# A graph layer on one core: units of picks that run on across groups, and a batch's copy in the middle of an iteration

## The chip, the cores and the metric

The kernel runs on one core of one Trainium2 chip. The metric is the device time of one execution in microseconds (us); the median of several executions is given, and a profile of one execution, taken apart from them, shows the work of the engines: PE (TensorE) multiplies matrices into PSUM, DVE (VectorE) and ACT (ScalarE) work elementwise, POOL (GpSimd) issues the gathers by index, and SP (SyncE) issues the other DMAs.

## The reference

There are N = 6250 nodes with 64 features, and E = 206250 edges sorted by destination. Four heads of 16 features each; every edge has its own 64 features.

```python
Qh = (x @ Wq.T + bq).reshape(n, H, D)
Kh = (x @ Wk.T + bk).reshape(n, H, D)
Vh = (x @ Wv.T + bv).reshape(n, H, D)
Ee = (edge_attr @ We.T + be).reshape(-1, H, D)
score = (Kh[src] * Qh[dst] * (1.0 / np.sqrt(D)) * Ee).sum(-1)
score = jnp.exp(jnp.clip(score, -5.0, 5.0))
msg = Vh[src] * score[..., None]
wV = jax.ops.segment_sum(msg, dst, num_segments=n)
...
x = _layernorm(x + wV.reshape(n, H * D))
```

So every edge needs the keys and values of its source, the query of its destination and its own projected features; its message is added to the row of its destination, and each row is normalised at the end.

## The kernel before

A prologue multiplies the nodes by the weights and writes a table of keys and values, a table of queries and a table of destination keys to DRAM. Then the edges run in tiles of 128, eight tiles to a group: 202 groups (NG), one iteration of the main loop (L1014) for each, and one more. Two groups make a step for the sums, but for the last eight.

**One iteration g, by engines.** VectorE multiplies keys by queries times edge values and reduces them to scores (`products`), multiplies edge values and queries of the next group (`terms`), adds the last step's sums into a ring of rows (`add`, in every other iteration; `add_blocks` now and then), builds one-hot matrices for the picks of the next iteration (`hots`), forms the message (`message`), and near the end the one-hots of the destinations (`onehot_edges`) and the message's low part (`take`). ScalarE turns scores to weights (`weigh`), adds the edge bias (`biased`, tile eb), copies the message's high part (`keep`), widens one-hots that VectorE wrote in bf16 (`widened`, pieces 1, 3 and 5 of 7) and prepares the one-hots for the queries of group g+4 (`onehot_rows`, `onehot_rows_rest`). PE turns the next group's terms (`turn`, four transposes into qe), multiplies the queries' one-hots (`queries`, into the bank qq), sums a step's messages (`sums`, into `pa`) and multiplies the edges of group g+3 (`edges`, into `ee`). SP fetches edges, keys, query windows, and index rows of sources; POOL gathers keys and values from the table by source index, each lot released by a mark in PE's order (list `where`).

**Picks.** Most tiles get their keys and values by the gather. Four tiles of a batch, two each in two later groups, get them by matmul instead: `picks` selects the sources' rows of x by one-hot matrices, and a product with the weights (`picked_kv`) makes keys and values of them. There are LAST = 78 batches. A batch goes through all nodes in 13 units of 512; a unit is two matmuls (high and low part) into each of two PSUM banks, px[0] and px[1]; the last unit is one into each. Two units make a piece, the seventh piece has one; `hots` makes a piece at a time, in a ring of six buffers. The first unit of a batch starts the accumulation in the banks, the last one ends it.

When a batch is complete, VectorE's `picked` (L722, L723) copies both banks to SBUF, tiles x0 and x1, and chooses by the source's low bits on the way. In the next iteration ScalarE fills the bank qq with the bias (`biased_kv`, L733), PE multiplies x0 and x1 by the weights into it (`picked_kv`), ScalarE copies the result out to the gathered tiles (`place_kv`, L739), and only then may `queries` use qq again.

**Order of the batches.** Batches last three and two iterations in turn (LENGTHS); BEGIN and READY hold each batch's first and last iteration. `pieces_of(g)` deals whole pieces to the iterations of a batch, 2, 2 and 3 pieces or 3 and 4, so that iterations have 4, 4, 5, 6 and 7 units and no iteration holds units of two batches. The loop's `todo` is the list of units of g and `ahead` the pieces of g+1.

In PE's order an iteration runs two units, the turn, the queries, then the other units with the sums between them (after the units where g is in READY), and the edge products at the end. Behind a READY iteration `picked_kv` follows the turn, and the queries come after the sums. `picked` stands at the very end of VectorE's order in a READY iteration, behind `onehot_edges` and `take`. `fetch_sources` (L252) brings the next batch's source indices to one buffer, one iteration before `sources` (two activations, L257 and L258, and a VectorE instruction, L259) turns them to what `hots` and `picked` read; `sources` stands at the end of a batch's first iteration.

**PSUM.** Eight banks: still (constants and a small sum), room (two banks in one tile: `ee` for the edge products, `pa` and `folded` for sums and folds in the other), px[0], px[1], qq, and qe twice. The program's semaphores follow its tiles.

Of the kernel before, what the change touches and what calls it, by code (L numbers as in the profile page):

```python
# [8 lines left out]
F32 = mybir.dt.float32  # L9
# [8 lines left out]
P = 128  # L18
# [79 lines left out]


def pieces_of(g):  # L100

    for m in range(LAST):
        if BEGIN[m] <= g <= READY[m]:
            n, k = READY[m] - BEGIN[m] + 1, g - BEGIN[m]
            return [(m, p) for p in range(len(PIECES) * k // n, len(PIECES) * (k + 1) // n)]
    return []

# [42 lines left out]
def tile_gnn(ctx: ExitStack, tc: tile.TileContext, x, x_blocks, by_rows, xT, wT, bias, beT, weT, eT, src, src_rows,  # L150
# [502 lines left out]
    with tc.If(rv == 0) as branch:  # L653

        with tc.tile_pool(name="work", bufs=2) as work, \
# [9 lines left out]
                                half_b[:2 * UNITS].to_broadcast([2 * UNITS, P]), ident_b[:2 * UNITS, :2 * UNITS])  # L665
            room = fixed.tile([P, 2, 4 * P], F32, name="room")
            ee = room[:, 0].rearrange("p (i e) -> p i e", e=P)
            pa = room[:, 1, :2 * PA]
            folded = room[:, 1, 2 * PA:2 * PA + 2 * C].rearrange("p (b c) -> p b c", c=C)
            sum_ = still[:, 2 * P:2 * P + C]  # L670
# [343 lines left out]
            for g in range(NG + 1):  # L1014
                now, before = g < NG, g > 0
                todo, ahead = [(m, p, u) for m, p in pieces_of(g) for u in range(*PIECES[p])], pieces_of(g + 1)
                going, where = [], []
# [8 lines left out]
                if g % LG == 0 and g + 3 * LG < NG:  # L1026
                    fetch_edges(g // LG + 3, work, 3)
                if g + 1 in BEGIN[1:]:
                    fetch_sources(BEGIN.index(g + 1) + 1, work)
                if g + 4 < NG:  # L1030
# [48 lines left out]
                if g - 1 in ends and now:  # L1079
# [3 lines left out]
                    else:  # L1083
                        short.append(lambda: sums(s))
                for k in range(max(len(todo), 3)):
                    for one in todo[k:k + 1]:
                        picks(*one)
                        where.append(mark[-1])
                    if k == 1:
                        if g + 1 < NG:  # L1090
                            turn(g + 1)
                        if g - 1 in READY:
                            picked_kv(READY.index(g - 1))
                            place_kv(READY.index(g - 1))
                        elif g + 2 < NG:
                            queries(g + 2)
                    if k in (2, 4) and short and g not in READY:
# [5 lines left out]
                if g + 3 < NG:  # L1103
# [218 lines left out]
```

## Time and profile before

| | |
|---|---|
| runs | 2001.13, 2002.62, 1995.0 us; median 2001.13 |
| profiled execution | 2019.47 us, of which the span of its instructions is 2017.7 us |
| mean granted TensorE clock | 0.932 |
| picks: units in five iterations | 4, 4, 5, 6, 7 |

One profile page tells busy time and idle time by engine and by group of instructions; a group's row has its busy time and the mean length of one, and then the idle time of its engine just before it and what ended that. The list of waits has in each row who waited for whom, the total, the number of times and the longest one. A timeline row begins with the start and the length. The ends of matmuls are modelled, and DMA-issuing instructions don't count as busy.

### The profile page before, as it was taken

The page shows a single profiled execution, that of the slowest core. Times are in us where ns is not written, and L with a number is a line of the kernel's source. Part 1 is how long each engine was busy: PE and PEld are TensorE (multiplying, and loading weights), DVE is VectorE, ACT ScalarE, POOL GpSimd, SP SyncE. Part 2 cuts the span into 40 slices and gives each one's busy share as a digit, 9 for nine tenths or more (in the row PEclk, how much of TensorE's full clock was granted, in tenths as well). Part 3 has the DMA queues.
Part 4 walks back from the last instruction along what each step waited for, and adds up shares of the span by engine and source line. Part 5 has one row for each costly group of instructions (what it writes and reads, how often), then busy time and mean ns, then how long its engine had stood idle before and what let it go on. Part 6 is the DMA issues. An engine that isn't in the chain of part 4 may idle for free.

```text
span 2017.7 us, 25692 instructions
## 1 busy us (share of the span) xinstructions
PE 1738.5 (86%) x7993; PEld 1259.1 (62%) x7993; DVE 1486.0 (74%) x2650; ACT 1328.1 (66%) x2047; POOL 1255.5 (62%) x1310
## 2 busy tenths in 40 slices
PE   6569989888888898979888989888888988889995
PEld 6346666666666665657566666666666666656664
DVE  5457777777777686878777777778777777678786
ACT  3456676676766676767667667667766667577674
POOL 6566666666666665666666666666666666666441
PEclk9789999999999998999899999999989999999996
DMA  6523333333333333333333333333333333333320
GB/s 178 190 90 114 100 103 103 98 97 100 93 108 101 91 102 88 102 115 99 93 97 92 107 104 93 104 90 103 101 88 114 104 95 104 97 93 98 97 71 20
DMA packets 116116, 203.70 MB, mean 101 GB/s; under 512 B 54784, under 2 KB 56425, under 8 KB 115855
## 3 DMA queue, kind: packets, MB, share of 16 engines
q1 hardware_dynamic: 73932, 116.94, 19.0%
q0 software_dynamic: 41600, 83.97, 14.7%
q10 hardware_dynamic: 436, 1.04, 0.2%
q8 instruction: 65, 1.06, 0.2%
q14 instruction: 83, 0.68, 0.1%
HBM read 194.25 MB, written 7.59 MB: 100 GB/s over the span
## 4 chain that ended last, share of the span: by engine, by line
PE 63%; DVE 16%; issue 7%; ACT 6%; another core or an unknown queue 4%; DMA 2%; POOL 1%; DVEq 0%; SPq 0%; ACTq 0%; POOLq 0%
PE pick L744 37%; PE room L744 10%; PE qq L744 10%; PE qe L775 4%; DVE hot L696 3%; DMA kv<-kv_tab,src_i 2%; DVE score L808 2%; DVE prod L806 1%; DVE qe L830 1%; DVE x L722 1%; DVE term L769 1%; POOL kv L295 1%; ACT kv L739 1%; DVE msg L850 1%
## 5 line engine op out<-in xcount | busy, mean ns | idle before, releaser
L295 POOL DMA_INDIRECT kv<-kv_tab,src_i x1260 | 1216.2, 965 | 708.8 <-issue 277.1
L744 PE MATMUL pick<-hot,parts 128*128 128x512 f32 x3900 | 1143.6, 436 | 115.5 <-DVE x L722 79.5
L744 PEld LDWEIGHTS pick<-hot,parts 128*128 128x128 f32 x3900 | 742.3, 198 | 418.8 <-issue 167.8
L696 DVE TENSOR_TENSOR hot<-from,still 128x1024 fp32r<-128x1024 bf16 x231 | 280.3, 1213 | 0.6 <-ACT from L257 0.6
L707 ACT ACTIVATE hot<-thin 128x1024 fp32r<-128x1024 bf16 x234 | 245.4, 1049 | 19.4 <-remote 19.3
L769 DVE TENSOR_TENSOR term<-eb,qq 128x512 f32<-128x512 f32 x202 | 137.3, 680 | 137.2 <-PE qq L744 98.1
L755 ACT ACTIVATE eb<-room,be_col 128x512 f32<-128x512 f32 x202 | 137.1, 679 | 148.2 <-DVE still L900 50.4
L744 PE MATMUL room<-et,we_sb 128*128 128x512 f32 x404 | 226.2, 642 | 7.5 <-ACT eb L755 6.2
L844 ACT ACTIVATE msg<-qe 128x512 fp32r<-128x512 f32 (+1 forms) x206 | 123.2, 598 | 157.5 <-DVE qe L830 74.4
L278 ACT ACTIVATE to<-to,one_p 126x1024 bf16<-126x1024 bf16 x198 | 225.7, 1140 | 0.1
L272 ACT ACTIVATE to<-kb,minus_row 126x1024 bf16<-126x1024 uint8 x198 | 225.2, 1137 | 0.0
L813 ACT ACTIVATE score<-score,five_p 128x32 f32<-128x32 f32 x203 | 64.1, 316 | 235.4 <-DVE score L808 144.6
L775 PE MATMUL qe<-ident,term 128*128 128x128 f32 x806 | 135.5, 294 | 58.9 <-DVE term L769 39.4
L775 PEld LDWEIGHTS qe<-ident,term 128*128 128x128 f32 x806 | 104.0, 151 | 111.9 <-DVE term L769 55.8
L744 PE MATMUL qq<-w,x 128*128 128x128 f32 x1248 | 165.8, 288 | 5.0 <-issue 3.6
L806 DVE TENSOR_TENSOR prod<-kv,qe 128x512 f32<-128x512 f32 x203 | 137.0, 675 | 43.1 <-remote 38.3
L830 DVE SCALAR_TENSOR_TENSOR qe<-weight,kv 128x512 f32<-128x512 f32 x200 | 139.8, 699 | 35.1 <-ACT weight L815 22.3
L722 DVE SCALAR_TENSOR_TENSOR x<-odd,upper,pick 128x512 f32<-128x512 int32 x77 | 57.3, 744 | 144.7 <-PE pick L744 115.2
L744 PEld LDWEIGHTS qq<-w,x 128*128 128x128 f32 x1248 | 155.6, 202 | 12.9 <-issue 8.0
L696 DVE TENSOR_TENSOR thin<-from,still 128x1024 bf16<-128x1024 bf16 x231 | 157.1, 680 | 0.0
L808 DVE TENSOR_REDUCE score<-prod 128x32 f32<-128x512 f32 x203 | 138.5, 682 | 7.0
L850 DVE TENSOR_TENSOR msg<-qe,msg 128x512 fp32r<-128x512 f32 x194 | 132.2, 681 | 2.9 <-ACT msg L844 1.4
(166 smaller groups left out, 1490.5 us busy)
## 6 DMA issues: line engine op xcount, KB each, us to landing
et<-in_eT SPq DMA_DIRECT2D x100, 512.0 KB
kb<-key_tab SPq DMA_DIRECT2D x101, 252.0 KB
kv<-kv_tab,src_i POOLq DMA_INDIRECT x1260
srcs<-in_src_rows SPq DMA_DIRECT2D x78, 256.0 KB
qw<-q_tab SPq DMA_DIRECT2D x202, 15.8 KB
kv_tab<-kv_sb SPq DMA_DIRECT2D x4, 640.0 KB
q_tab<-q SPq DMA_DIRECT2D x5, 480.0 KB
out<-y SPq DMA_DIRECT2D x2, 512.0 KB
```

The costliest lines, as they stand in the source:

```text
L272: nc.scalar.activation(TO[g][:, :n, :], KB.pop(g)[:, :n * P].rearrange("p (j e) -> p j e", j=n), AF.Square, bias=minus_row3[:3 * W])
L278: nc.scalar.activation(TO[g][:, :n, :], TO[g][:, :n, :], AF.Relu, bias=one_p[:3 * W], scale=-1.0)
L295: return nc.gpsimd.indirect_dma_start(out=kv_of(g)[:, j, :], out_offset=None, in_=kv_tab[:, :], in_offset=bass.IndirectOffsetOnAxis(ap=src ...
L696: nc.vector.tensor_tensor(to.rearrange("p b (a c) -> p b a c", c=2), pairs((FROM if hi < UNITS else OVER)[m])[:, None].to_broadcast(shape) ...
L707: nc.scalar.activation(*THIN.pop(0), AF.Copy)
L744: mark.append(nc.tensor.matmul(*aps, **kw))
L769: nc.vector.tensor_mul(TERM[g][:, :n], EB.pop(g)[:, :n], qq[:, :n])
L775: nc.tensor.transpose(qe[g % 2][:, 2 * k:2 * k + 2, :], TERM[g][:, k, :], ident)
L806: nc.vector.tensor_mul(prod, kv_of(g)[:, lo:hi, :C], qe[g % 2][:, lo:hi, :])
L808: nc.vector.tensor_reduce(SCORE[g], prod.rearrange("p g (h d) -> p g h d", h=H), axis=AX.X, op=OP.add)
L830: nc.vector.scalar_tensor_tensor(to.rearrange("p g (h d) -> p g h d", h=H), WEIGHT.pop(g)[:, :, :, None].to_broadcast([P, n, H, D]), LEAST ...
L850: nc.vector.tensor_sub(part_of(g, 1)[1], left, part)
```

## The change

The units of all batches become one stream, and iterations take 4, 6, 6, 4 and 6 of it in turn (the first one takes one more). Batches still end in the same iterations, but within them: of six units in a READY iteration two or five end a batch (`head`), and the rest begin the next one. With a head of two, its picks come first in the iteration and `picked` follows `add_blocks` in VectorE's order, ahead of the one-hots and the message; then PE has turn, queries, sums and edge products, and then the four units of the next batch. With a head of five, the turn stands after the second unit; queries, sums and edge products follow the fifth, then `picked`, and then one unit of the next batch. Everything that belongs to the sources moves one iteration ahead: the fetch to the iteration before READY, `sources` to the end of READY. The tile room is split into ee and room, one bank each.

```diff
+FLOW = 4, 6, 6, 4, 6
+STREAM = [(m, p, u) for m in range(LAST) for p, piece in enumerate(PIECES) for u in range(*piece)]
+UPTO = [0] * (LEAD + 1)
+for g in range(LEAD, NG):
+    UPTO.append(UPTO[-1] + FLOW[(g - LEAD) % len(FLOW)] + (g == LEAD))
...
+def units_of(g):
+    return STREAM[UPTO[g]:UPTO[g + 1]] if g < NG else []
 def pieces_of(g):
-    for m in range(LAST):
-        if BEGIN[m] <= g <= READY[m]:
-            n, k = READY[m] - BEGIN[m] + 1, g - BEGIN[m]
-            return [(m, p) for p in range(len(PIECES) * k // n, len(PIECES) * (k + 1) // n)]
-    return []
+    return [(m, p) for m, p, u in units_of(g) if u == PIECES[p][0]]
+SOURCES = {LEAD: 1, **{r: m + 2 for m, r in enumerate(READY)}}
+FETCHES = {r - 1: m + 2 for m, r in enumerate(READY)}
...
-            room = fixed.tile([P, 2, 4 * P], F32, name="room")
-            ee = room[:, 0].rearrange("p (i e) -> p i e", e=P)
-            pa = room[:, 1, :2 * PA]
+            ee = fixed.tile([P, G // 2, P], F32, name="ee")
+            room = fixed.tile([P, 4 * P], F32, name="room")
+            pa = room[:, :2 * PA]
...
-                if g + 1 in BEGIN[1:]:
-                    fetch_sources(BEGIN.index(g + 1) + 1, work)
+                if g in FETCHES:
+                    fetch_sources(FETCHES[g], work)
...
                 if g - 1 in FOLDS:
                     add_blocks(FOLDS[g - 1])
+                if 0 < len(head) <= 3:
+                    for one in head:
+                        picks(*one)
+                        where.append(mark[-1])
+                    picked(ending)
...
-                for k in range(max(len(todo), 3)):
+                for k, one in enumerate(head if len(head) > 3 else []):
+                    picks(*one)
+                    where.append(mark[-1])
+                    if k == 1 and g + 1 < NG:
+                        turn(g + 1)
+                if head:
+                    if len(head) <= 3 and g + 1 < NG:
+                        turn(g + 1)
+                    if g + 2 < NG:
+                        queries(g + 2)
+                    while short:
+                        short.pop(0)()
+                    if g + 3 < NG:
+                        edges(g + 3)
+                    if len(head) > 3:
+                        picked(ending)
+                    for one in todo[len(head):]:
+                        picks(*one)
+                        where.append(mark[-1])
+                for k in range(0 if head else max(len(todo), 3)):
...
-                if g in BEGIN:
-                    sources(BEGIN.index(g) + 1, *from_odd())
+                if g in SOURCES:
+                    sources(SOURCES[g], *from_odd())
...
-                if g in READY:
-                    picked(READY.index(g))
```

More of the change, by code (lines that the diff above doesn't have):

```diff
@@ L97 @@
 READY = [begin(m + 1) - 1 for m in range(LAST)]
-def pieces_of(g):
-    for m in range(LAST):
-        if BEGIN[m] <= g <= READY[m]:
-            n, k = READY[m] - BEGIN[m] + 1, g - BEGIN[m]
-            return [(m, p) for p in range(len(PIECES) * k // n, len(PIECES) * (k + 1) // n)]
-    return []
+FLOW = 4, 6, 6, 4, 6
[3 more added lines that the diff above has]
+    UPTO.append(UPTO[-1] + FLOW[(g - LEAD) % len(FLOW)] + (g == LEAD))
+assert UPTO[NG] >= len(STREAM)
+assert all(UPTO[r] < (m + 1) * UNITS <= UPTO[r + 1] for m, r in enumerate(READY))
+def units_of(g):
+    return STREAM[UPTO[g]:UPTO[g + 1]] if g < NG else []
+def pieces_of(g):
+    return [(m, p) for m, p, u in units_of(g) if u == PIECES[p][0]]
+SOURCES = {LEAD: 1, **{r: m + 2 for m, r in enumerate(READY)}}
+FETCHES = {r - 1: m + 2 for m, r in enumerate(READY)}
 PICKED = [(r + k, r + k + 1) for r in READY for k in [min(4, NG - 2 - r - 1)]]
@@ L665, in tile_gnn @@
                                 half_b[:2 * UNITS].to_broadcast([2 * UNITS, P]), ident_b[:2 * UNITS, :2 * UNITS])
-            room = fixed.tile([P, 2, 4 * P], F32, name="room")
-            ee = room[:, 0].rearrange("p (i e) -> p i e", e=P)
-            pa = room[:, 1, :2 * PA]
-            folded = room[:, 1, 2 * PA:2 * PA + 2 * C].rearrange("p (b c) -> p b c", c=C)
+            ee = fixed.tile([P, G // 2, P], F32, name="ee")
+            room = fixed.tile([P, 4 * P], F32, name="room")
+            pa = room[:, :2 * PA]
+            folded = room[:, 2 * PA:2 * PA + 2 * C].rearrange("p (b c) -> p b c", c=C)
             sum_ = still[:, 2 * P:2 * P + C]
@@ L1015, in tile_gnn @@
                 now, before = g < NG, g > 0
-                todo, ahead = [(m, p, u) for m, p in pieces_of(g) for u in range(*PIECES[p])], pieces_of(g + 1)
+                todo, ahead = units_of(g), pieces_of(g + 1)
+                ending = READY.index(g) if g in READY else None
+                head = [one for one in todo if one[0] == ending]
                 going, where = [], []
@@ L1096, in tile_gnn @@
                             queries(g + 2)
-                    if k in (2, 4) and short and g not in READY:
+                    if k in (2, 4) and short:
                         short.pop(0)()
@@ L1102, in tile_gnn @@
                     queries(g + 2)
-                if g + 3 < NG:
+                if g + 3 < NG and not head:
                     edges(g + 3)
```

## The prediction

> **What bounds the kernel now.** I read the page first: the engines' busy line, the chain that ended last and the costliest groups. Times are in us, means of one instruction in ns.
>
> ```profile
> span 2017.7 us, 25692 instructions
> ...
> PE 1738.5 (86%) x7993; PEld 1259.1 (62%) x7993; DVE 1486.0 (74%) x2650; ACT 1328.1 (66%) x2047; POOL 1255.5 (62%) x1310
> ...
> PE 63%; DVE 16%; issue 7%; ACT 6%; another core or an unknown queue 4%; DMA 2%; POOL 1%; DVEq 0%; SPq 0%; ACTq 0%; POOLq 0%
> ...
> L744 PE MATMUL pick<-hot,parts 128*128 128x512 f32 x3900 | 1143.6, 436 | 115.5 <-DVE x L722 79.5
> ```
>
> PE is the bound: 86% busy, 63% of the chain, and well over half of its busy time is the picks. But it is not full: some 280 of 2018 are idle, and the largest single piece of that, 79.5, stands before picks and ends when VectorE's copy x (L722, then L723) has emptied the pick banks. The list of waits says how often that happens, that the same copy waits for the picks in turn, and which other wait lies close to the change:
>
> ```profile
> DVE x L722 <- PE pick L744: 115.2, 42, 5.1
> ...
> PE pick L744 <- DVE x L722: 79.5, 23, 6.0
> ...
> PE qq L744 <- ACT kv L739: 44.0, 32, 4.4
> ```
>
> Of the 78 batches 23 make PE stand still for x, 3.5 each. PE's timeline shows where, and what follows (first the end of a batch of three iterations and the iteration behind it, then one that ends a batch of two):
>
> ```profile
> 998.25 1.02 PE L744 MATMUL room<-et,we_sb 128*128 128x512 f32 x2
> 1002.61 3.78 PE L744 MATMUL pick<-hot,parts 128*128 128x512 f32 x8 [3.34 <-DVE x L722]
> 1006.19 1.05 PE L775 MATMUL qe<-ident,term 128*128 128x128 f32 x4
> 1007.04 2.48 PE L744 MATMUL qq<-w,x 128*128 128x128 f32 x16
> ...
> 1015.93 2.43 PE L744 MATMUL pick<-hot,parts 128*128 128x512 f32 x8
> 1018.20 0.60 PE L775 MATMUL qe<-ident,term 128*128 128x128 f32 x4
> 1018.72 0.41 PE L744 MATMUL qq<-to,qw 126*64 126x512 bf16 x2
> 1019.06 4.48 PE L744 MATMUL pick<-hot,parts 128*128 128x512 f32 x18
> ```
>
> After the edge products (room<-et) PE has nothing but picks, and those need the banks: 3.34 idle. Then eight picks take 3.78 where eight take 2.43 elsewhere, and the turn (qe) 1.05 instead of 0.60. Two windows show that the clock is down in that stretch:
>
> ```profile
> 1001.00:1008.00 7.00, 5.39 (x17) 4.47 (x18) 6.97 (x12) 5.98 (x10) 5.17 (x7) 0.52 0.28 84
> ...
> 1016.00:1023.00 7.00, 7.00 (x33) 5.22 (x32) 5.12 (x11) 3.92 (x5) 4.39 (x5) 1.00 0.56 168
> ```
>
> The columns are the stretch, its length, the busy time of PE, weight loads, VectorE, ScalarE and GpSimd, then the granted clock and the DMA. In 7.00 at 0.52 PE starts 17 matmuls, at 1.00 it starts 33.
>
> **The change part by part.** *Picks and copy.* Units no longer stop at a batch's end. In the ending iteration the head (two units of a long batch, five of a short one) comes first, then turn, queries, sums and edge products, then the tail: units of the next batch, which need the banks. VectorE's copy moves from behind the one-hot work at the iteration's end to its middle. The 79.5 go if the copy is done by the tail: −79.5. With them goes the slow stretch: 3.78 − 2.43 and 1.05 − 0.60 make 1.8 per stall, 41 for 23. Other idle pieces remain and may pull the clock down as well; between half of it and all, I take −35.
>
> [...]
>
> *What is late next: the tail.* The durations that decide it, from the groups by line:
>
> ```profile
> L696 DVE TENSOR_TENSOR hot<-from,still 128x1024 fp32r<-128x1024 bf16 x231 | 280.3, 1213 | 0.6 <-ACT from L257 0.6
> ...
> L696 DVE TENSOR_TENSOR thin<-from,still 128x1024 bf16<-128x1024 bf16 x231 | 157.1, 680 | 0.0
> ...
> L830 DVE SCALAR_TENSOR_TENSOR qe<-weight,kv 128x512 f32<-128x512 f32 x200 | 139.8, 699 | 35.1 <-ACT weight L815 22.3 <-issue 6.0 <-ACT wide L797 2.0
> L808 DVE TENSOR_REDUCE score<-prod 128x32 f32<-128x512 f32 x203 | 138.5, 682 | 7.0
> L769 DVE TENSOR_TENSOR term<-eb,qq 128x512 f32<-128x512 f32 x202 | 137.3, 680 | 137.2 <-PE qq L744 98.1 <-ACT to L278 15.4 <-ACT score L813 5.3
> L755 ACT ACTIVATE eb<-room,be_col 128x512 f32<-128x512 f32 x202 | 137.1, 679 | 148.2 <-DVE still L900 50.4 <-DVE y L957 40.1 <-remote 11.7
> L806 DVE TENSOR_TENSOR prod<-kv,qe 128x512 f32<-128x512 f32 x203 | 137.0, 675 | 43.1 <-remote 38.3 <-PE pick L744 2.5 <-issue 0.6
> ```
>
> ```profile
> L900 DVE TENSOR_REDUCE still<-room 64x64 f32<-64x128 f32 x194 | 58.0, 299 | 87.8 <-PE qq L744 41.8 <-PE pick L744 17.0 <-PE room L744 8.6
> L722 DVE SCALAR_TENSOR_TENSOR x<-odd,upper,pick 128x512 f32<-128x512 int32 x77 | 57.3, 744 | 144.7 <-PE pick L744 115.2 <-remote 29.5
> L723 DVE SCALAR_TENSOR_TENSOR x<-odd,upper,pick 128x512 f32<-128x512 int32 x77 | 57.1, 741 | 0.0
> L257 ACT ACTIVATE from<-srcs,from_row 128x512 bf16<-128x512 int32 x77 | 55.5, 720 | 0.0
> L258 ACT ACTIVATE over<-srcs,last_row 128x512 bf16<-128x512 int32 x77 | 55.2, 717 | 0.0
> L696 DVE TENSOR_TENSOR hot<-over,still 128x512 fp32r<-128x512 bf16 x77 | 52.4, 680 | 0.0
> L739 ACT ACTIVATE kv<-qq 128x256 f32<-128x256 f32 x156 | 50.9, 379 | 64.9 <-PE pick L744 35.2 <-remote 18.4 <-PE room L744 9.5
> ```
>
> Between head and tail PE has turn 0.60, queries 0.41 and edge products 1.02, so 2.0; the copy's two halves take 1.5. A head of two units is six matmuls at 4.48/18 = 0.25, so 1.5. VectorE comes to the copy only after prod, score and term (2.0), and in every other iteration after the add's two reductions (0.6) and two ring updates, no longer than those: 3.2. If it starts along with PE it is late by up to 1.7, less the 0.5 by which PE's cover is longer than the copy: 1.2, 39 times. With a head of five (18 matmuls and the turn, 5.1) it has besides a normal and a thin one-hot (1.2 and 0.7) and the message (0.7), 5.8 in all: late by 0.7, 39 times. Together 0 to 74. VectorE is 26% idle and can run ahead, so I take a third: +25. Queued behind the waiting copy on VectorE are one-hots for the next iteration and, with a two-unit head, the message; ScalarE's split of the message waits for that, and PE meets the one-hots one iteration later.
>
> *What is late next: the product bank.* In the iteration behind a batch's end ScalarE fills qq with the bias, PE multiplies into it, ScalarE copies it out (L739), and only then may the queries run: 44.0 of waiting now. Two edits make this tighter. Behind a long batch this iteration has four units instead of six, so 8 × 0.25 = 2.0 of cover are gone, 39 times: 78. And the sources (L257, L258: 1.44) move from the end of this iteration to the end of the one before it, ahead of ScalarE's work for the bank, 78 times: 112. Bounds 0 and 190. Against the upper end stands that ScalarE is idle 34% and that L739 itself waited 64.9 for others, so much of what moves ahead of it fills idle time. Nearer to the lower end, I take +45.
>
> *The split bank.* room becomes two tiles of a bank each. Now ScalarE's eb, which reads only the edge half, waits 50.4 for the reductions and 40.1 for the fold's add, which read the other half. These waits go. PE hardly stands for eb, so they are worth between nothing and the 44.0 at the product bank, which an earlier ScalarE could shorten; I take −5.
>
> *At nothing.* The one-hots stay as many: 3, 3, 2, 4, 2 pieces per iteration instead of 2, 3, 3, 4, 2. The fetch of the sources on SP's queue moves one iteration ahead together with its reader; it has one buffer, so SP may wait there for ScalarE, with query windows and keys queued behind it that are due two iterations later. Were that slack gone, the queries would be late by as much. POOL's gathers are still released by PE's marks.
>
> Sum: −79.5 − 35 + 25 + 45 − 5 = −49.5 on the profiled execution's 2019.5 (span 2017.7 and 1.8 around it): 1970.0. The median of the runs is 2001.13, 0.991 of the profiled time: 1970.0 × 0.991 = **1952**.
>
> **The rivals.** *All clears (0.17).* The clock stays up and nothing is taken back: −79.5 − 41 and some 9 of eb's make 1890, at the median 1873. For it: VectorE and ScalarE have the idle time. Against it: both are tied to PE's progress and uneven from one iteration to the next. [...]
>
> *The wait only moves (0.12).* The two costs come to some 110 to 130 instead of 70 and eat the gain: 2000. For it: 42 of the copies wait for picks now, and will wait for heads.
>
> *The product bank becomes the stall (0.21).* In the iteration behind each batch PE stands before the queries until L739 has run. The gain without this is 79.5 + 35 − 25 = 89.5, so it is lost from 89.5/78 = 1.15 per batch on. At three quarters of the bound, 143, the sum is +48.5: 2068, at the median 2049. For it: the longest of these waits is 4.4 already, and four units are little cover for a chain of bias, products and copy. Against it: only 32 of 78 wait now.
>
> **How the numbers follow.** My forecast has 0.50. Its own range comes from the two costs at 27 or 108 instead of 70: 1910 to 1990. With the rivals the range is 1860 to 2045; that leaves out the outer part of the first and of the last. Under 0.5% (10 us) counts as the same, about what a measurement here can tell. Faster is the forecast and the first rival, 0.67; the same 0.12; slower 0.21.
>
> **What would show it.** Right: "PE pick <- DVE x" falls from 79.5 to under 30, fewer stretches at half clock are left, eb no longer waits for still and y, and "PE qq <- ACT kv" grows from 44.0 towards 90. First rival: that last wait does not grow. Third rival: it passes 130. I am wrong in the main step if PE stands before the tail for x as long as before, or if what it gains there comes back as idle time before instructions that the change did not touch.

## The result, and the profile after

The kernel after the change took 2022.94 us (median of 4 runs, 2020.91 to 2024.82), the kernel before 1998.07 beside it (1991.77 to 2002.62): a ratio of 1.012, with a 95% interval of 1.0097 to 1.0143. It is slower by 1.2%, where 1952 was forecast. The profiled execution took 2023.11, only 3.6 longer than that of before, which lay 21 above its own median; so the two traces show less of the difference than the runs do.

The page after: the span, the busy line, the shares of the chain that ended last, and three groups of PE (busy time and mean ns, then the idle time just before and what ended it).

```profile
span 2021.3 us, 25665 instructions
...
PE 1723.2 (85%) x7993; PEld 1263.6 (63%) x7993; DVE 1486.7 (74%) x2650; ACT 1324.8 (66%) x2047; POOL 1261.0 (62%) x1310
...
PE 49%; ACT 18%; DVE 15%; issue 10%; another core or an unknown queue 5%; DMA 2%; SPq 1%; DVEq 0%; ACTq 0%; POOL 0%
...
L758 PE MATMUL pick<-hot,parts 128*128 128x512 f32 x3900 | 1108.3, 429 | 21.3 <-issue 12.8
...
L758 PE MATMUL qq<-w,x 128*128 128x128 f32 x1248 | 183.9, 309 | 46.0 <-ACT qq L747 32.9
...
L758 PE MATMUL qq<-to,qw 126*64 126x512 bf16 x396 | 84.3, 418 | 112.8 <-ACT kv L753 89.4
```

The idle time before picks fell from 115.5 to 21.3, as the change would have it. But the picked products (qq<-w,x) now have 46.0 before them and the queries (qq<-to,qw) 112.8, where the same groups of before had 5.0 and 48.5:

```profile
L744 PE MATMUL qq<-w,x 128*128 128x128 f32 x1248 | 165.8, 288 | 5.0 <-issue 3.6
...
L744 PE MATMUL qq<-to,qw 126*64 126x512 bf16 x396 | 83.9, 418 | 48.5 <-ACT kv L739 44.0 <-issue 2.3 <-DMA kb<-key_tab 2.1
```

So 94 went at one bank and 105 came at another. Over the whole span PE's busy time fell by 15.3 and its idle time grew by 18.9. In the chain ScalarE's share grew from 6% to 18%. The list of waits (who waited for whom, total, times, longest) names the new ones:

```profile
ACT msg L858 <- DVE qe L844: 145.3, 68, 6.8
...
PE qq L758 <- ACT kv L753: 89.4, 34, 6.4
ACT kv L753 <- remote: 73.8, 17, 6.6
...
PE qq L758 <- ACT qq L747: 32.9, 22, 2.2
...
PE pick L758 <- DVE x L736: 8.3, 8, 2.4
```

Three rows matter later. ScalarE's split of the message (msg) waits 145.3 for VectorE, twice as long as before:

```profile
ACT msg L844 <- DVE qe L830: 74.4, 82, 1.6
```

PE waits for the bias in the product bank (ACT qq L747), a wait that the list of before doesn't have. And ScalarE's copy out of that bank (kv) waits 73.8 for "remote": work whose end the trace can't name. The timeline of PE, and then that of ScalarE, shows one of those 17:

```profile
474.94 2.05 PE L758 MATMUL qq<-w,x 128*128 128x128 f32 x16 [0.35 <-issue]
476.75 2.11 PE L758 MATMUL pick<-hot,parts 128*128 128x512 f32 x8
485.31 0.64 PE L758 MATMUL qq<-to,qw 126*64 126x512 bf16 x2 [6.45 <-ACT kv L753]
```

```profile
477.00 1.05 ACT L721 ACTIVATE hot<-thin 128x1024 fp32r<-128x1024 bf16 x1
484.60 0.66 ACT L753 ACTIVATE kv<-qq 128x256 f32<-128x256 f32 x2 [6.55 <-remote]
```

PE is through with the picked product at 476.99 (by the modelled ends) and with all its picks at 478.86; ScalarE is free from 478.05. Yet kv starts at 484.60, and the queries behind it at 485.31. Nothing runs on PE for 6.45. The records of PE's semaphore say the same: for some microseconds none comes, though matmuls that set it have ended by the modelled ends, and then a bunch comes within 0.3. Such a bunch is called a held mark here. Counting bunches of two or more behind a stretch of over 1.2 without a record, whose first matmul had ended about a microsecond before, the trace of before has some 135, that of after some 130; counted from the ends of their first matmuls they make about 410 and 350 in sum. (Where the line is drawn moves the counts by ten or so. With three or more in a bunch there are some 100 in each; the expectations below use that count.) Two things limit this reading. Ends of matmuls are modelled, so a mark that comes late and a matmul that ends late look alike. And in these traces many semaphore records are missing: of the changed kernel's 2405 PE marks 1983 are recorded, of VectorE's 2407 only 1338, of ScalarE's 1722 only 933. So whether other engines' marks are held too can't be told.

### The profile page after: what moved, and what is told of

It reads as the page before. It is cut to its first block, busy times and chain, and to the rows that moved or that the text cites. A ratio compares the mean times of both kernels' runs of the same rounds, so it can differ in the third digit from the quotient of the medians.

```text
span 2021.3 us, 25665 instructions
## 1 busy us (share of the span) xinstructions
PE 1723.2 (85%) x7993; PEld 1263.6 (63%) x7993; DVE 1486.7 (74%) x2650; ACT 1324.8 (66%) x2047; POOL 1261.0 (62%) x1310
## 4 chain that ended last, share of the span: by engine, by line
PE 49%; ACT 18%; DVE 15%; issue 10%; another core or an unknown queue 5%; DMA 2%; SPq 1%; DVEq 0%; ACTq 0%; POOL 0%
PE pick L758 26%; PE qq L758 9%; PE ee L758 7%; ACT hot L721 4%; PE room L758 4%; PE qe L789 3%; ACT to L286 2%; DVE hot L710 2%; ACT to L292 2%; DVE x L737 2%; ACT msg L858 2%; DVE prod L820 1%; DVE score L822 1%; PE ps L527 1%
## 5 line engine op out<-in xcount | busy, mean ns | idle before, releaser
L758 PE MATMUL pick<-hot,parts 128*128 128x512 f32 x3900 | 1108.3, 429 | 21.3 <-issue 12.8
L858 ACT ACTIVATE msg<-qe 128x512 fp32r<-128x512 f32 (+1 forms) x206 | 122.6, 595 | 259.8 <-DVE qe L844 145.3
L783 DVE TENSOR_TENSOR term<-eb,qq 128x512 f32<-128x512 f32 x202 | 137.4, 680 | 170.1 <-PE qq L758 116.9
L721 ACT ACTIVATE hot<-thin 128x1024 fp32r<-128x1024 bf16 x234 | 246.0, 1051 | 11.6 <-remote 5.5
L758 PE MATMUL ee<-et,we_sb 128*128 128x512 f32 x404 | 236.7, 670 | 6.8 <-ACT eb L769 5.7
L758 PE MATMUL qq<-w,x 128*128 128x128 f32 x1248 | 183.9, 309 | 46.0 <-ACT qq L747 32.9
L769 ACT ACTIVATE eb<-ee,be_col 128x512 f32<-128x512 f32 x202 | 136.7, 677 | 124.6 <-PE ee L758 42.0
L758 PEld LDWEIGHTS qq<-w,x 128*128 128x128 f32 x1248 | 170.0, 219 | 59.1 <-ACT qq L747 41.5
L789 PE MATMUL qe<-ident,term 128*128 128x128 f32 x806 | 126.8, 281 | 64.6 <-DVE term L783 41.0
L758 PE MATMUL qq<-to,qw 126*64 126x512 bf16 x396 | 84.3, 418 | 112.8 <-ACT kv L753 89.4
L789 PEld LDWEIGHTS qe<-ident,term 128*128 128x128 f32 x806 | 98.1, 143 | 110.7 <-DVE term L783 57.7
```

Of the source, the lines that this page charges most:

```text
L721: nc.scalar.activation(*THIN.pop(0), AF.Copy)
L758: mark.append(nc.tensor.matmul(*aps, **kw))
L783: nc.vector.tensor_mul(TERM[g][:, :n], EB.pop(g)[:, :n], qq[:, :n])
L789: nc.tensor.transpose(qe[g % 2][:, 2 * k:2 * k + 2, :], TERM[g][:, k, :], ident)
L858: nc.scalar.activation(part, left, AF.Copy)
```

## The experiments

Three theories. T1: what x gained was given back at the product bank, because the bias for it comes late (the sources moved ahead of it) and few units stand in front of the queries. T2: the copy x, ahead of the message in VectorE's order with a two-unit head, makes ScalarE wait for the message, and everything behind it late. T3: the marks of PE that come late fall on whatever round trip is short of cover (the work that PE has in front of a wait), and decide both kernels. (In the first expectation below T3 is another theory, that the split of the tile makes the rest of the difference.)

The runs fell on several chips, and this turned out to matter more than any edit. Beside runs 5 to 8 the kernel before took 2015.6, much as in the first result, and all four traces of these runs have some 130 to 140 held marks. Beside all others it took 1785 to 1786, on four chips; the traces of those runs have no bunch of three or more and at most three of two, and their semaphore records are all but complete (2394 of PE's 2405 and 1720 of ScalarE's 1722 in the changed kernel's). "Without held marks" means these. The kernel before itself was traced only where marks are held. Ratios are always to the kernel before on the same chip.

| kernel | ratio, without held marks | ratio, with held marks |
|---|---|---|
| changed | 1.002 [1.0009, 1.0031] | 1.012 [1.0097, 1.0143]; 1.0108 [1.0054, 1.0162] |
| before, bank split only | 0.9936 [0.9923, 0.9949] | |
| changed, product in ee | 1.0068 [1.0053, 1.0084] | |
| changed, sources late | 1.0242 [1.0229, 1.0255] | |
| changed, message first | 0.9651 [0.9638, 0.9663]; 0.9633 [0.9616, 0.965]; 0.9647 [0.963, 0.9665] | |
| message first, 5 5 6 4 6 | 0.9628 [0.961, 0.9645] | 1.0124 [1.009, 1.0158] |
| message first, one tile | | 1.0128 [1.0094, 1.0162] |
| changed, 4 4 6 6 6 | 0.9678 [0.9665, 0.9692] | 1.0073 [1.0049, 1.0096] |

**The split alone.**

```diff
 (before)
+            ee = fixed.tile([P, G // 2, P], F32, name="ee")
+            room = fixed.tile([P, 4 * P], F32, name="room")
```

> The kernel before with the tile room split into ee and room and nothing else. T1 (what the copy gained was given back at the product bank) expects little of the split itself: eb's waits for still (50.4) and y (40.1) vanish, the time stays within 0.5% of before (1988 to 2008). T3 (the split moves ScalarE's work and so the rest of the difference) expects 0.8% or more in either direction.

1773.8 against 1785.4: a gain of 0.64%, just beyond what T1 allowed, below the 0.8 of the theory that stands there as T3. The more telling thing is what this kernel, otherwise the one of before, waits for without held marks:

```profile
PE qq L744 <- ACT kv L739: 25.0, 19, 1.5
...
PE pick L744 <- DVE x L722: 12.7, 15, 2.1
```

The wait of 79.5 that the change was costed by is 12.7 here, and 16.6 in the kernel before with one tile and without gathers (below), also without held marks. So over 60 of it comes only where marks are held.

**Product in the edge products' bank.**

```diff
 (changed)
-            rooms = qq.rearrange("p i e -> p (i e)").rearrange("p (j c) -> p j c", j=BATCH)
+            rooms = ee.rearrange("p i e -> p (i e)").rearrange("p (j c) -> p j c", j=BATCH)
...
+                        if g + 2 < NG:
+                            queries(g + 2)
                         if g - 1 in READY:
                             picked_kv(READY.index(g - 1))
                             place_kv(READY.index(g - 1))
-                        elif g + 2 < NG:
-                            queries(g + 2)
```

> The changed kernel with the picked product in the bank of the edge products instead of that of the queries, so that no query waits for a picked product; the edge products behind a batch wait for it instead. T1 expects the idle time of PE before queries and picked products to fall from 112.8 + 46.0 to under 70, and 60 to 90 us less than the changed kernel: 1930 to 1965, faster than before. T2 (the copy ahead of the message starves ScalarE, and everything behind is late) expects the wait to go on, at the edge products or at the turn, and 0 to 30 us less: 1990 to 2023. T3 (PE's marks are held back, wherever it stands) expects 2010 to 2030.

(The edit also puts the edge bias ahead of the bank's bias in ScalarE's order.) It took 1799.4, 0.5% more than the changed kernel on such a chip, where T1 expected a gain of 3 to 4.5%. The queries wait no longer, but, as T2 had it, the waits go on at the edge products: for the bias in the bank, and for kv.

```profile
PE ee L758 <- ACT ee L747: 53.0, 52, 2.5
...
PE ee L758 <- ACT kv L753: 17.5, 19, 1.1
```

**Sources late.**

```diff
 (changed)
-SOURCES = {LEAD: 1, **{r: m + 2 for m, r in enumerate(READY)}}
-FETCHES = {r - 1: m + 2 for m, r in enumerate(READY)}
+SOURCES = {LEAD: 1, **{r + 1: m + 2 for m, r in enumerate(READY)}}
+FETCHES = {r: m + 2 for m, r in enumerate(READY)}
...
+                for piece in deferred:
+                    hots(*piece)
```

> The changed kernel with the sources' fetch and their two activations back where they stood before, one iteration later, behind the picked product instead of ahead of it. T1 in its first half (the sources stand ahead of the bias for the bank) expects the bias 1.44 earlier behind each batch: the wait of picked products for the bias falls from 32.9 to under 10, and the time by 30 to 60 us, to 1963 to 1993. If the four units of cover are what matters, the wait for kv stays at 89 and the time falls by under 20. T2 expects under 20 as well.

1828.9, 2.2% worse than the changed kernel, which no theory had. Its wait for the bias did fall to 14.0, but one one-hot of every other batch now stands behind the sources, and VectorE waits for them with the term queued behind it:

```profile
DVE hot L710 <- ACT from L271: 128.6, 38, 4.1
PE qe L789 <- DVE term L783: 113.6, 69, 6.0
```

So the sources' move to an earlier iteration is not a mere cost: the tail's first one-hots need it. T1's first half was not tested cleanly.

**Message first.**

```diff
 (changed)
                     for one in head:
                         picks(*one)
                         where.append(mark[-1])
-                    picked(ending)
...
                 if now:
                     message(g, *some_of(g)[0])
+                if 0 < len(head) <= 3:
+                    picked(ending)
```

> The changed kernel with the copy of a two-unit head moved behind the message in VectorE's order. T2 expects the wait of ScalarE's msg for VectorE's qe to fall from 145.3 to 75 to 100 and the time by 20 to 50 us (1973 to 2003), unless picks of the tail wait longer for x (23.8 now). T1 expects within 15 us of the changed kernel (2008 to 2030), with the wait for kv near 89.

1723.0, or 0.9651 of before. The absolute times expected for these four were meant for a chip like the first; as a ratio, T2's 1973 to 2003 is a gain of 1 to 2.5% on the changed kernel. How that one does on a chip of this kind was run later (1.002); against it this is a gain of 3.7%, the way T2 expected and more than it had.

**The changed kernel once more, and three variants: a chip with held marks.** The other edits are FLOW = 4, 4, 6, 6, 6; message first with FLOW = 5, 5, 6, 4, 6; message first with room in one tile again.

> The changed kernel itself, once more, beside the kernel before on the same chip. The chip of the first four runs took 1785 for the kernel before where the first one took 1998, and none of their traces shows PE's marks held back, of which the first chip's trace of before has 105 and that of after 100, 1 to 6 us each. T1 (the product bank gives the gain back wherever the kernel runs) expects 1.00 to 1.02 on a chip like that too, with some 100 us idle before queries and picked products. T2 (the message behind the copy) expects 0.985 to 1.005, above the 0.965 of the kernel with the message first, with msg waiting over 100 more than there. T3 (the holds of the first chip fall on waits with less cover) expects 0.965 to 0.98 here, next to the kernel with the message first, and 1.01 only where the trace shows holds.

> The changed kernel with 4, 4, 6, 6, 6 units: six instead of four behind a long batch, and every ending iteration takes the path of the long heads (four or five units), in which the copy stands behind the message. T1 (too little cover behind a long batch) expects the waits for kv and for the bias at that place to go, and 20 to 40 us less than the changed kernel. T2 expects the same or more, since the copy ahead of the message is gone as well: 30 to 60 less. If neither matters, within 10 of the changed kernel.

> The kernel with the message first, with 5, 5, 6, 4, 6 units: five instead of four behind a short batch, where its trace has all of the 26.7 that queries still wait for kv (19 times, 1.4). A unit is 8 x 0.25 = 2.0 of cover, so the wait goes wholly: 20 to 27 less than the kernel with the message first, 0.950 to 0.955 of before, unless the term becomes the bound there.

> The kernel with the message first, with ee and room in one tile again as before. The split alone gave 0.9936 of before. If its worth is the same here, 0.970 to 0.974; if VectorE's reductions and fold stand beside the edge products more tightly now, 0.975 to 0.985 with eb waiting for still and y; under 0.967 if the split does nothing here.

The times were 2043.0, 2031.6, 2045.3 and 2041.9 against 2015.6. The first result repeats (1.0108), and the other orders give nothing either: 4 4 6 6 6 is 11 below the changed kernel where T1 and T2 had 20 to 60, and the two with the message first are at 1.012 and 1.013, where 0.950 to 0.955 and 0.970 to 0.985 were expected. What the one tile costs can't be told on this chip. The waits of message first with one tile, then of 4 4 6 6 6:

```profile
PE qq L758 <- ACT kv L753: 90.4, 38, 5.7
...
ACT kv L753 <- remote: 80.6, 25, 6.3
```

```profile
DVE x L736 <- remote: 87.0, 18, 7.1
PE pick L758 <- DVE x L736: 85.3, 31, 6.7
...
PE qq L758 <- ACT kv L753: 22.2, 14, 5.4
```

In the first the copy kv waits for marks that come late, and the queries for kv. With six units behind a long batch that goes down to 22.2, as T1 had it for more cover. But then it is the copy x that waits for late marks (87.0), and the tail for x (85.3). Going by these traces, each order moves the loss to the round trip from PE to another engine and back that has least in front of it.

**The changed kernel and message first on one chip without held marks.**

> The changed kernel once more beside the kernel before. On a chip without held marks T3 (the holds, which fall on any wait that is left) expects 0.965 to 0.985 of before; T1 (the product bank gives the gain back wherever it runs) expects 1.00 to 1.02. On a chip with some 100 holds both expect 1.005 to 1.015.

> The changed kernel with the message ahead of the copy. On a chip without held marks it took 0.965 of before, and should again (0.962 to 0.968). On a chip with some 100 holds T3 expects 1.00 to 1.015, as for its two variants with 55646 units and with one tile; T2 (VectorE's order starves ScalarE) expects 0.975 to 0.995 there too.

1789.1 and 1722.4 against 1785.8: 1.002 and 0.963. For the changed kernel T1's figure holds, and T3's does not: even without a held mark the change gains nothing. But T1's place is only the end of the chain, and the one edit that makes the difference, 66.7, is T2's. The waits of the changed kernel, then of message first:

```profile
ACT msg L858 <- DVE qe L844: 234.4, 143, 3.8
...
DVE x L736 <- PE pick L758: 103.8, 75, 2.8
...
PE qq L758 <- ACT qq L747: 33.2, 20, 2.1
...
PE qq L758 <- ACT kv L753: 28.3, 19, 1.6
```

```profile
ACT msg L858 <- DVE qe L844: 143.6, 163, 2.1
...
PE qq L758 <- ACT kv L753: 26.8, 19, 1.6
```

The chain can be read in an iteration with a two-unit head and the one behind it. In the changed kernel VectorE, ScalarE and PE, in that order:

```profile
776.33 0.75 DVE L736 SCALAR_TENSOR_TENSOR x<-odd,upper,pick 128x512 f32<-128x512 int32 x1 [1.81 <-PE pick L758]
...
777.65 1.21 DVE L710 TENSOR_TENSOR hot<-from,still 128x1024 fp32r<-128x1024 bf16 x1
778.90 0.70 DVE L844 SCALAR_TENSOR_TENSOR qe<-weight,kv 128x512 f32<-128x512 f32 x1
```

```profile
779.63 0.60 ACT L858 ACTIVATE msg<-qe 128x512 fp32r<-128x512 f32 x1 [3.78 <-DVE qe L844]
...
785.89 0.58 ACT L747 ACTIVATE qq<-bkv_all 128x512 f32<-128x512 f32 x1
```

```profile
783.81 0.60 PE L789 MATMUL qe<-ident,term 128*128 128x128 f32 x4
786.53 3.62 PE L758 MATMUL qq<-w,x 128*128 128x128 f32 x16 [2.12 <-ACT qq L747]
```

VectorE waits 1.81 for the head's picks with the one-hot and the message queued behind the copy. ScalarE therefore stands idle for 3.78. From there to the bias it has no gap: row one-hots, widening, sources, weights, one after the other. So the bias comes late, PE stands for 2.12, and the product then takes 3.62. With the message first, the same place:

```profile
752.40 0.70 DVE L844 SCALAR_TENSOR_TENSOR qe<-weight,kv 128x512 f32<-128x512 f32 x1
753.05 0.75 DVE L736 SCALAR_TENSOR_TENSOR x<-odd,upper,pick 128x512 f32<-128x512 int32 x1
```

```profile
753.14 0.60 ACT L858 ACTIVATE msg<-qe 128x512 fp32r<-128x512 f32 x1 [0.58 <-DVE qe L844]
...
759.83 0.58 ACT L747 ACTIVATE qq<-bkv_all 128x512 f32<-128x512 f32 x1
```

```profile
760.53 0.60 PE L789 MATMUL qe<-ident,term 128*128 128x128 f32 x4
760.97 1.95 PE L758 MATMUL qq<-w,x 128*128 128x128 f32 x16
```

The copy x, which PE needs only after turn, queries and edge products, no longer waits; the message goes out at once; ScalarE is idle for 0.58 and has the bias ready before PE is through with the turn. The product takes 1.95. The spans differ by 65.2: 41.2 less idle time on PE, of which 34.2 before the products, and 24.0 less busy time, at a granted clock of 0.982 instead of 0.973.

**Where the held marks come from.** Two kernels with work left out.

```diff
 (before, no gathers)
-                for i, lot in enumerate(going):
+                for i, lot in enumerate(going if g < 20 else []):
 (before, half the picks)
-                for k in range(2):
+                for k in range(2 if u in (0, UNITS - 1) or u % 2 else 0):
```

> The kernel before without the gathers of keys and values from iteration 20 on (later groups read what lies in the buffers), so without 1100 of GpSimd's 1260 indirect DMAs and some 73 of the 204 MB. If PE's marks are held because of GpSimd's descriptors or the gathers' traffic, a chip on which the other kernels show some 100 holds shows under 20 after iteration 20, and the time comes to 1760 to 1800. If the holds have nothing to do with them, 80 to 110 are left and the time stays at 1960 to 2020. On a chip without holds 1740 to 1790 and no holds.

> The kernel before with every other unit's picks left out (the first unit, the odd ones and the last one remain, so x is wrong). PE has some 450 us less to do, and VectorE's 1480 becomes the bound: 1550 to 1650 on a chip without holds. If the marks are held at a constant rate of PE's busy time (7.5 in 100 us in the traces of before and after), a chip with holds shows 80 to 95 of them; if they come from PE's sustained load, fewer than 40.

They fell on chips without held marks, and so did every repeat:

> The changed kernel with the message ahead of the copy, 0.963 and 0.965 of before on two chips without held marks. On a chip with some 100 holds T3 expects 1.00 to 1.015 of before, as its variants with 55646 units and with one tile had there; if the two variants were the cause and not the holds, 0.97 to 0.99. On a chip without holds again 0.963 to 0.965.

> Message first with five units instead of four behind a short batch. On a chip without holds the 26.8 of queries that wait for kv go: 0.948 to 0.953 of before, or 0.960 to 0.965 if the term takes their place. On a chip with some 100 holds 1.005 to 1.02 as before.

> The kernel before without gathers from iteration 20 on; on a chip without holds it took 1781.0 against 1785.8, so the gathers cost nothing there. On a chip with some 100 holds: if GpSimd's descriptors or that traffic hold the marks, under 20 holds after iteration 20 and 1780 to 1820; if not, 80 to 110 holds and 1960 to 2020.

> The kernel before with every other unit's picks left out (x is wrong); 1674.5 on a chip without holds. On a chip with some 100 holds: 75 to 95 holds if they come at a constant rate of PE's busy time, fewer than 40 if they come from PE's sustained load; and if waits with slack in front of them swallow the holds, under 100 us more than without them, where the full kernel has 215 to 230 more.

> The kernel before without gathers from iteration 20 on, 1781 on two chips without holds. On a chip with some 100 holds: if the gathers hold the marks, under 20 holds after iteration 20 and 1780 to 1820; if not, 80 to 110 holds and 1960 to 2020. On a chip without holds 1778 to 1785 and none.

No gathers took 1781.0, 1781.5 and 1783.6, so the gathers cost the kernel at most 0.3% there. Half the picks took 1674.5 and 1666.7, above the 1550 to 1650 expected; PE is 82% busy there and VectorE 89%. Neither says where the marks are held up. Message first again gave 0.9647. Five units behind a short batch took the wait of queries for kv from 26.8 to 9.2. All of it was expected to go, but by an error: a unit is four picks, 1.0 of cover and not 2.0, and 19 times 1.0 is about the 17.6 that went. The time fell only from 1722.7 to 1720.1 (0.9628): the turn's wait for the term grew from 43.9 to 48.0, and the rest isn't accounted for.

**The same order by another way.**

> The changed kernel with 4, 4, 6, 6, 6 units, 1.007 of before on a chip with holds. On a chip without them: every ending iteration copies behind the message, and six units stand behind a long batch. T2 (the copy ahead of the message is what gives the gain back) expects 0.955 to 0.97, as for the message-first kernel (0.963 to 0.965), with under 5 idle before the picked product. T1 (cover behind the batch) expects no more than that, but with the waits for kv at 26.8 unchanged, since behind a short batch there are still four units. If what the message-first kernel gains comes from something else than that order, 0.985 to 1.005. On a chip with holds 1.005 to 1.01 again.

1729.3 against 1784.8, 0.9678: in the range of T2. With heads of four and five the copy always stands behind the message. The two waits at the bank:

```profile
PE qq L758 <- ACT kv L753: 8.9, 19, 0.6
...
PE qq L758 <- ACT qq L747: 5.2, 11, 0.7
```

The 8.9 is below the 26.8 that T1 expected to stay, so that part was wrong; the 5.2 before the picked product is just above the 5 that T2 allowed. The kernel still isn't faster than message first, which waits longer there.

How the idle time of PE moves among the three places, from the groups by line of each trace:

| kernel | picks | picked products | queries | sum |
|---|---|---|---|---|
| with held marks: before | 115.5 | 5.0 | 48.5 | 169.0 |
| changed, first result | 21.3 | 46.0 | 112.8 | 180.1 |
| changed, again | 26.8 | 41.1 | 116.9 | 184.8 |
| 4 4 6 6 6 | 124.5 | 3.6 | 35.4 | 163.5 |
| message first, 5 5 6 4 6 | 65.8 | 5.1 | 97.1 | 168.0 |
| message first, one tile | 49.3 | 2.4 | 115.9 | 167.6 |
| without: before, split | 12.7 | 2.2 | 25.0 | 39.9 |
| changed | 0.0 | 34.7 | 28.3 | 63.0 |
| message first | 0.6 | 0.5 | 26.9 | 28.0 |
| 4 4 6 6 6 | 1.0 | 5.2 | 8.9 | 15.1 |

With held marks six traces have 164 to 185, whatever the order. Without them the order decides, and the changed kernel is the worst of the four. (The three places aren't all of PE's idle time, which is 279 in the trace of before and 298 in the first of the changed kernel.)

## Why the prediction was wrong, point by point

*Picks and copy, −79.5 and −35.* The wait for x did go: 8.3 is left, under the 30 named as the sign. But the step that failed is the one that read those 79.5 as a wait of this schedule that vanishes when the copy is in time. With no held mark it is 12.7 to 16.6; the rest comes with late marks, and these come about as often after the change (some 130 for 135). What they cost then shows at other short round trips.

The trace of before shows how they make up the 79.5. In 6 of the 23 stalls the copy x itself waits for a late mark ("remote", 29.5 in 7 waits). In the other 17 it waits for nothing: VectorE comes to it late, and in 16 of these because the reduction of the sums (still<-room), some six microseconds ahead of the copy, had waited 1.5 to 4.8 for PE. The stall that the prediction shows is one of them. VectorE there, and then VectorE and PE at the same place of the kernel with one tile and without gathers, where no mark is held:

```profile
995.98 0.64 DVE L900 TENSOR_REDUCE still<-room 64x64 f32<-64x128 f32 x2 [2.56 <-PE qq L744]
...
1001.82 0.74 DVE L722 SCALAR_TENSOR_TENSOR x<-odd,upper,pick 128x512 f32<-128x512 int32 x1
```

```profile
856.72 0.63 DVE L900 TENSOR_REDUCE still<-room 64x64 f32<-64x128 f32 x2
...
862.56 0.74 DVE L722 SCALAR_TENSOR_TENSOR x<-odd,upper,pick 128x512 f32<-128x512 int32 x1
```

```profile
863.35 2.33 PE L744 MATMUL pick<-hot,parts 128*128 128x512 f32 x8 [0.71 <-DVE x L722]
```

By the modelled ends the sums of the first were through at 992.39 and the edge products, in the other half of the same tile, at 993.25; four of PE's marks came together between 995.88 and 996.07. With 2.56 of waiting there, PE's gap behind the copy is 3.34; without, 0.71. These stalls are no scattered accidents: 19 of the 23 stand at the end of every second long batch, some 95 apart. So nothing in their rhythm set them apart from a wait of the schedule; only VectorE's own last wait did. The idle time before that reduction fell from 87.8 to 23.0 with the change (53.9 when it was run again), and the change also split its tile. The split alone was not run where marks are held, so how much of the 79.5 went by it and how much by the copy's move isn't known.

The −35 was too large as well: the picks alone gave that much (1143.6 to 1108.3), but the picked products, now behind new gaps, took 18.1 more (165.8 to 183.9, 288 ns to 309 each), and PE's whole busy time fell by only 15.3 (1738.5 to 1723.2).

The prediction tied the slow stretches to the stalls before x, 3.34 in the one it shows, and put 35 of their 41 down as gone with these. The stalls went and the slow stretches did not: the trace of before has 42 stretches at a granted clock of 0.50, that of after 44, at a mean of 0.932 and 0.938. Long gaps came elsewhere (6.45 before the queries shown above), and shorter ones have such a stretch behind them too. The windows of the changed kernel on a chip without held marks, on either side of the gap of 2.12 shown above:

```profile
777.80:783.80 6.00, 6.00 (x26) 4.60 (x25) 5.93 (x10) 4.17 (x6) 4.48 (x6) 1.00 0.29 83
786.50:790.00 3.50, 3.47 (x17) 3.47 (x18) 3.50 (x6) 3.05 (x4) 2.31 (x3) 0.53 0.66 173
```

The clock is 1.00 in the 6.00 of the first and 0.53 in the 3.50 of the second. Not every such gap is followed by a fall of the clock: of the gaps that PE came to at full clock in the main loop of this trace, 8 of the 11 of 2.0 to 2.2 are, within 3.5 of their end, and 1 of the 12 of 1.5 to 2.0; in the first trace of the changed kernel 11 of 15 and 7 of 15. Of the 39 gaps of 3.0 or more that it came to at full clock in the main loops of the first traces of before and after, 38 are. Going by these counts, the shorter gaps must be priced too.

*The tail, +25.* Of its two halves one was put too high: PE waits 8.3 for x, its weight loads 23.8. The other was seen and not priced: "ScalarE's split of the message waits for that" is just what happens: 74.4 became 145.3, and without held marks it is 234.4 against the 143.6 of message first. It ends at PE before the picked products, and without held marks undoing it is worth 66.7 (1789.1 to 1722.4).

*The product bank, +45.* This is the term of the sum that was most mis-sized. Idle time before queries grew by 64.3 and before products by 41.0, 105.3 together. The second of these, PE waiting for the bias, stood nowhere in the prediction: it priced the sources ahead of the bias, but took ScalarE's idle third as a buffer. In the iteration shown that idle time lies before the message; behind it ScalarE runs without a gap up to the bias. Of the 105.3, 28.3 + 34.7 − 25.0 − 2.2 = 35.8 come without held marks, against the split kernel of before; the rest came only with them.

*The split bank, −5.* Right in kind: eb no longer waits for still or y. Its size was more: 0.64%, 11.6 of 1785, without held marks; with them it isn't known.

*The rivals.* "The product bank becomes the stall" was nearest, with 1.15 per batch as the point from which the gain is lost; 105.3/78 is 1.35. But its sign, "PE qq <- ACT kv" over 130, did not come (89.4), because the second wait at that bank was not in it. By the sign for the forecast, 44.0 growing "towards 90", one would have called the main line right. The last sentence of the prediction was the better test: what was gained came back as idle time before instructions that the change did not touch.

*What stays open.* Why marks are held, and why only on some chips (or at some times on them), isn't settled. The traces with held marks are also the ones that lack semaphore records, nearly half of VectorE's and ScalarE's; whether the recording itself has a part in the delays, or only suffers from the same cause, no run here tells. Gathers and PE's load could not be tried where it happens. Nor is it settled why the orders that are 3 to 4% faster without them are no faster with them: message first with 5 5 6 4 6 loses 325 to them (1720.1 to 2045.3) and 4 4 6 6 6 302 (1729.3 to 2031.6), where the changed kernel loses 254 (1789.1 to 2043.0) and before 230 (1785.8 to 2015.6). That the loss moves with the cover was seen in the waits; that a fuller schedule must lose more per held mark is only argued. Message first itself was not met on such a chip.

## What to carry to other kernels

Before a wait is put into a sum, follow the engine that it waits for back to that engine's own last wait. Here PE mostly waited for a copy that itself waited for nothing, but stood behind a reduction that had waited for late marks of PE; such a wait can come back elsewhere once this place is gone, however regular it looks (19 of 23 stood in one rhythm). And trace the kernel on more than one chip: the 79.5 of one was 12.7 and 16.6 in two near relatives on others. When a step that can wait moves up in an engine's order, price the steps behind it by following their consumers all the way back to the bound engine: here one waiting copy ahead of the message cost 66.7, and moving it two instructions down made the fastest kernels of this study on chips without held marks (0.963 to 0.965 of before). No version here beat the kernel before on a chip with them; the nearest, 4 4 6 6 6, was 0.7% slower.

## What the hardware showed that was not expected

The same program took 1785 on four chips and 1998 to 2016 in two other measurements, and the difference is not the clock alone (0.932 in the trace of before, 0.984 for its split version without held marks): of the 248.8 between these two spans, 160.5 is idle time of PE and 88.3 busy time. In the six traces of the slower kind PE's semaphore goes silent some 130 to 140 times, for about 3 on average by the modelled ends, and then gives several marks within 0.3; the number is about the same for all five kernels traced there. The records of semaphores are incomplete in these six traces and all but complete in the others. A sign of it in the list of waits is "remote" as the releaser of waits for PE: 73.8 before ScalarE's kv in both traces of the changed kernel there, and none in its trace on a chip without held marks. The second surprise is the clock: around one gap of PE of 2.12 it was 1.00 before and 0.53 in the 3.50 behind, and it fell within 3.5 after 8 of 11 gaps of 2.0 to 2.2 in that trace and after 11 of 15 in the first one of the changed kernel.
